# Expert rows in three rounds instead of five parts: tiles that later parts go on filling

## The chip, the cores and the metric

The kernel runs on one core of a Trainium2 chip. The metric is the device time of one execution in microseconds (us). Three timed runs of the kernel before took 2634.92, 2636.18 and 2640.61 us; the median is 2636.18. "Before" is the kernel as it stands, "after" the changed one.

## What is computed

A layer of a graph network (attention over edges), then a layer of a mixture of experts. There are 6250 nodes with 256 features, 206,250 edges sorted by their target, and 16 experts, of which each node uses two. Cut to what matters:

```python
def gnn(x, edge_index, W, a_src, a_dst, gamma, beta):
    hh = (x @ W).reshape(n, 8, 32)
    scores = leaky_relu(s_src[src] + s_dst[dst], 0.2)
    alpha = exp(scores - m[dst]) / denom[dst]
    out = segment_sum(hh[src] * alpha[:, :, None], dst) .reshape(n, 256) + x
    return elu(layernorm(out) * gamma + beta)

def ffn(x, gate_w, gate_b, w1, b1, w2, b2, gamma, beta):
    topk_vals, topk_idx = top_k(x @ gate_w + gate_b, 2)
    topk_w = softmax(topk_vals)
    h = relu(einsum('bsh,ehf->bsef', x, w1) + b1)         # 256 -> 512
    expert_out = einsum('bsef,efh->bseh', h, w2) + b2      # 512 -> 256
    y = x + sum(topk_w * take(expert_out, topk_idx))
    return layernorm(y) * gamma + beta

x = x + gnn(layernorm(x), edges, ...)
x = x + ffn(layernorm(x), ...)
```

## The kernel before, in words

Nodes are cut into 49 blocks of 128, edges into 52 chunks of 31 tiles of 128 edges. A short first stage computes a table row for each node (features, and two exponentials of its scores) and writes it to memory. Then comes one long loop over the 52 chunks, with three kinds of work in it.

*Edges.* A chunk is done in four groups of 8, 8, 8 and 7 edge tiles. GpSimd (POOL in the profile) issues one indirect gather for each edge tile (L188, tile `hx`); `hx` has four buffers, one per group. VectorE (DVE) makes two one-hot tiles (`oh` L864, `ohT` L871), TensorE (PE) fetches the targets' factors with them (`pm`, L879), VectorE weighs the gathered rows (`uv`, L887 to L892, `hx`, L895), and TensorE sums them over the edges (`agg`, L898, 32-bit). At the end of a chunk ScalarE (ACT) copies the sum (`carry`, L912) and stores it (L914). The copies of `carry` therefore mark the chunks in the trace.

*Node blocks.* When a chunk is done, the blocks whose edges are all in are finished by `node_block` (L543): attention output, two layer norms, the row `acc` that goes to the experts, the gate's logits and the top two experts. A table made beforehand says after which chunk a block is due.

*Experts.* The 49 blocks are taken in five parts that end at blocks 14, 26, 35, 43 and 49 (`PARTS`, L30). When the last block of a part is done, at the end of chunks 15, 27, 37, 45 and 51, `part_due` (L823) calls `routing` (L597). Routing counts, with one-hot tiles on VectorE and two matmuls on TensorE (L643, copied out by ScalarE, L644), how many rows each expert gets, rounds each count up to whole tiles of 128, and gives each pair (node, expert) a row (`pos`, L690) and each tile an expert (`owner`, L703). A part of n blocks has 2n + 15 tiles, the most that 2n full tiles of rows can need with 16 experts; that is 43, 39, 33, 31 and 27, together 173. Each part has its own row buffers in memory, `xg` for inputs and `yg` for outputs.

The work of the experts is then spread over the loop: after every group the function `some` (L809) issues at most four scatters of rows (`scatter`, L707, by GpSimd, into `xg`), then one step of biases (`biases`, L719: the gates' shares times `b2`, through TensorE, ScalarE, TensorE and VectorE into `acc`), and moves a pipeline of three tiles one step on: `weights` (L731: read the tile's expert into a register of SyncE, load its rows `xr`, `w1s`, `b1s`), `turned` (L743: load `w2s`, transpose the rows), `hidden` (L754: first matmuls, L758, and relu, L767) and `rows_out` (L770: second matmuls, L773, copy `yr`, L775, store into `yg`, L776). A tile is not begun before all scatters of its part are issued, and its row load waits for all of them. SyncE (SP) issues all the loads in one order, ScalarE the stores. A tile loads 1 MB of weights. `clear` (L534) fills the rows of one part with zeros in each of the first five chunks.

After the loop the tiles that are left are drained, and `result` (L778) gathers each node's two output rows from `yg`, adds them, and writes the result.

A scheduler puts the instructions of all this into one order for each engine; each engine then works through its own order. It does not keep to the order of the program: the 28 scatters of the first part, which the program has after the groups of chunks 16 and 17, stand in one run in GpSimd's order, after the first group of chunk 18's gathers. Small results on TensorE share one PSUM buffer, `pt` in the pool `wk` (`bufs=1`): routing, biases, node blocks and the transposes of the rows all go through it.

Of the kernel before, what the change touches and what calls it, by code (L numbers as in the profile page):

```python
# [20 lines left out]
P = 128  # L21
# [7 lines left out]
SLACK = 24  # L29
PARTS = (14, 26, 35, 43, 49)  # L30


@with_exitstack
def kernel(
# [39 lines left out]
    DUMP = (NB + 1) * P  # L74
    parts = list(zip((0,) + PARTS[:-1], PARTS))
    MTS = [2 * (hi - lo) + E - 1 for lo, hi in parts]
    assert LAST < P and N % P and NE > (NK - 1) * CE and PARTS[-1] == NB

# [8 lines left out]
    accd = dram.tile([(NB + 2) * P, RA], F32, name="accd")  # L87
    xg = [dram.tile([mt * P, C], F32, name=f"xg{i}") for i, mt in enumerate(MTS)]
    yg = [dram.tile([mt * P, C], F32, name=f"yg{i}") for i, mt in enumerate(MTS)]

# [414 lines left out]

    prep.close()


    v8 = const.tile([P, NB, 8], F32, name="v8")
    i8 = const.tile([P, NB, 8], U32, name="i8")  # L510
    nc.vector.tensor_scalar_add(fb, fb, -1.0)
    pos = [const.tile([P, NB], I32, name=f"pos{k}") for k in range(2)]
    gate = [const.tile([P, NB], F32, name=f"gate{k}") for k in range(2)]
    owner = [const.tile([1, mt], I32, name=f"owner{i}") for i, mt in enumerate(MTS)]
    b2r = const.tile([E, C], F32, name="b2r")
    nc.sync.dma_start(b2r, b2)
    tri = const.tile([P, P], F32, name="tri")
    nc.vector.tensor_scalar(tri, irow, nodes[:, 0:1], None, op0=ALU.is_gt)
    mtm = max(MTS)
    jt = const.tile([1, mtm], F32, name="jt")  # L520
    nc.gpsimd.iota(jt, pattern=[[1, mtm]], base=0, channel_multiplier=0, allow_small_or_imprecise_dtypes=True)
    with tc.tile_pool(name="w2", bufs=2) as w2_, tc.tile_pool(name="w3", bufs=3) as w3_, tc.tile_pool(
# [10 lines left out]

        def clear(i):  # L534

            for t in range(0, MTS[i], ZR):
                n = min(ZR, MTS[i] - t)
                nc.sync.dma_start(
                    xg[i][t * P : (t + n) * P, :].rearrange("(p j) c -> p j c", p=P),
                    zero[:, None, :].to_broadcast([P, n, C]),  # L540
                )
# [55 lines left out]
        def routing(i):  # L597

            lo, hi = parts[i]
            nb = hi - lo  # L600
# [51 lines left out]
            if nb > 1:  # L652
                nc.vector.tensor_add(place, place, incl)
                nc.vector.tensor_sub(place, place, own)


            mult = rt.tile([P, nb], F32, name="mult")
            nc.vector.tensor_scalar_mul(mult, irow[:, :nb], float(P))
            gtm = rt.tile([P, E, nb], F32, name="gtm")
            nc.vector.tensor_tensor(  # L660
                gtm,
                incl[:, nb - 1, :].unsqueeze(2).to_broadcast([P, E, nb]),
                mult[:, None, :].to_broadcast([P, E, nb]),
# [6 lines left out]
            while step < E:  # L670
# [4 lines left out]
            tiles_to = cur  # L675
            first_row = rt.tile([P, E], F32, name="first_row")
            nc.vector.tensor_sub(first_row, tiles_to, nt)
            nc.vector.scalar_tensor_tensor(
                place,
                first_row[:, None, :].to_broadcast([P, nb, E]),  # L680
                float(P),
                place,
                op0=ALU.mult,
                op1=ALU.add,
            )
            for k in range(2):
# [5 lines left out]

            mt = MTS[i]
            le = rt.tile([1, mt, E], F32, name="le")
            nc.vector.tensor_tensor(
                le,
                tiles_to[:1, None, :].to_broadcast([1, mt, E]),
                jt[:, :mt, None].to_broadcast([1, mt, E]),
                ALU.is_le,
            )  # L700
            of = rt.tile([1, mt], F32, name="of")
            nc.vector.tensor_reduce(of, le, AX.X, ALU.add)
            nc.vector.tensor_scalar_min(owner[i], of, float(E - 1))  # L703

        scattered = [[] for _ in parts]

        def scatter(i, b, k):  # L707
            n = P if b < NB - 1 else LAST
            t = nc.gpsimd.indirect_dma_start(  # L709
                out=xg[i][:, :],  # L710
                out_offset=bass.IndirectOffsetOnAxis(ap=pos[k][:n, b : b + 1], axis=0),
                in_=acc[:n, b, :],
                in_offset=None,
            )
            for o in scattered[i]:
                tc.declare_no_dep(t.ins, o.ins, reason="each pair has a row of its own")
            scattered[i].append(t)

# [9 lines left out]

        taken = []

        def weights(i, j):  # L731

            after = taken[-3] if len(taken) > 2 else ()
            e = load(owner[i][:, j : j + 1], 0, E - 1, engines=(ET.SP,), after=after)
            xr = e2.tile([P, C], F32, name="xr")
            nc.sync.dma_start(xr, xg[i][j * P : (j + 1) * P, :])
            w1s = e2.tile([P, KC, F], F32, name="w1s")
            nc.sync.dma_start(w1s, w1[ds(e, 1)].rearrange("a (k p) f -> p (a k) f", p=P))
            b1s = e2.tile([P, FC], F32, name="b1s", bufs=3)
            nc.sync.dma_start(b1s, b1d[ds(e, 1)].rearrange("a p f -> (a p) f"))  # L740
            return i, j, e, w1s, b1s, xr
# [28 lines left out]
        def rows_out(i, j, w2s, hT):  # L770
            po = wk.tile([P, C], F32, name="po")
            for f in range(FC):
                nc.tensor.matmul(po, lhsT=hT[:, f, :], rhs=w2s[:, f, :], start=(f == 0), stop=(f == FC - 1))  # L773
            yr = e2.tile([P, C], F32, name="yr")
            nc.scalar.copy(yr, po)  # L775
            nc.scalar.dma_start(yg[i][j * P : (j + 1) * P, :], yr)  # L776

        def result(i, b):  # L778
# [5 lines left out]
            for k in range(2):  # L784
                got = e2.tile([P, C], F32, name=f"got{k}", bufs=3)
                with tc.issue_after(scattered[-1][-1].ins):
                    nc.gpsimd.indirect_dma_start(  # L787
                        out=got[:n],
                        out_offset=None,
                        in_=yg[i][:, :],  # L790
                        in_offset=bass.IndirectOffsetOnAxis(ap=pos[k][:n, b : b + 1], axis=0),
                    )
# [29 lines left out]

        def part_due(i):  # L823
            routing(i)
            lo, hi = parts[i]
            scat.extend((i, b, k) for b in range(lo, hi) for k in range(2))
            bias.extend((i, b) for b in range(lo, hi))
            due.extend((i, j) for j in range(MTS[i]))

# [21 lines left out]
        for k in range(NK):  # L851
# [64 lines left out]
            for b in when.get(k, ()):  # L916
                node_block(b)
                for i, (lo, hi) in enumerate(parts):
                    if b == hi - 1:
                        part_due(i)  # L920
            if k < len(parts):
                clear(k)
        while scat or due or bias or any(at):
            some()
        for i, (lo, hi) in enumerate(parts):
            for b in range(lo, hi):
                result(i, b)
# [33 lines left out]
```

## Time and profile before

| | |
|---|---|
| median of the timed runs | 2636.18 us |
| the profiled execution | 3281.45 us |
| its span, first to last instruction | 3279.4 us |
| mean granted TensorE clock in it | 0.796 |
| moved by DMA | 592.51 MB, mean 181 GB/s |
| first gather to last `carry` | the loop, from about 99 to 2928 us |
| from there to the end | the drain, about 350 us |

The profiled execution is longer than the timed runs; its times are used for shares and for the cost of single steps. A line of a group reads: source line, engine, operation, output<-inputs, count | busy time in us, mean ns of one | idle time of the engine just before them and what ended it. "issue" means that nothing in the profile was waited for, "remote" that the profile cannot name who ended the wait. The ends of matmuls are modelled. A line of stretches reads: begin:end, length, then for each engine the busy time and the number of instructions.

### The profile page before, as it was taken

What the parts mean: (1) busy time and instruction counts of PE and PEld (TensorE: products, weight loads), DVE (VectorE), ACT (ScalarE), POOL (GpSimd) and SP (SyncE); (2) the same over time, 40 slices, a digit from 0 to 9 for tenths busy, and PEclk for the clock granted to TensorE, in tenths of its full rate; (3) what the DMA queues carried; (4) which work ended last, traced back from release to release, by engine and by line L of the source; (5) the groups of instructions that cost most, each with busy time, mean ns of one, the idle gap of its engine ahead of it and who ended that gap; (6) DMA issues with size and microseconds to landing.
All of it is one profiled execution on the core that took longest, in us unless ns stands there. A gap on an engine that the chain in (4) does not pass through costs nothing. (4 is left out here: it accounts for less than half of the span.)

```text
span 3279.4 us, 34441 instructions
## 1 busy us (share of the span) xinstructions
PE 2002.3 (61%) x10215; PEld 1614.8 (49%) x10215; DVE 1585.7 (48%) x3057; ACT 498.2 (15%) x1771; POOL 1759.4 (54%) x1867
## 2 busy tenths in 40 slices
PE   7344445454424877777636677747677657765565
PEld 5233333343323656666525566645466545654454
DVE  6445555465534444554625456445355524544431
ACT  4000000000000211111101111111111111122232
POOL 3665665666675445655555465664455645515501
PEclk9676777777767888888768888977789868887788
DMA  7875443444443657776546667755576746656896
GB/s 189 249 235 157 119 123 109 121 112 121 120 146 112 198 173 213 224 220 211 150 115 192 184 210 213 231 165 174 161 214 207 216 145 194 200 164 212 259 269 203
DMA packets 415255, 592.51 MB, mean 181 GB/s; under 512 B 104295, under 2 KB 304701, under 8 KB 415061
## 3 DMA queue, kind: packets, MB, share of 16 engines
q1 hardware_dynamic: 268968, 276.81, 28.5%
q0 software_dynamic: 89904, 263.85, 27.8%
q10 hardware_dynamic: 56188, 49.56, 4.4%
q8 instruction: 84, 1.38, 0.2%
q14 instruction: 111, 0.90, 0.1%
HBM read 504.00 MB, written 86.02 MB: 180 GB/s over the span
## 5 line engine op out<-in xcount | busy, mean ns | idle before, releaser
L188 POOL DMA_INDIRECT hx<-table,src_sb x1612 | 1537.3, 954 | 1153.8 <-issue 432.3
L898 PE MATMUL agg<-hx,oh 128*128 128x264 f32 x3224 | 977.3, 462 | 382.1 <-DVE hx L895 222.2
L898 PEld LDWEIGHTS agg<-hx,oh 128*128 128x128 f32 x3224 | 719.8, 231 | 552.1 <-DVE hx L895 233.8
L773 PE MATMUL po<-w2s,hT 128*128 128x256 f32 x1384 | 414.5, 444 | 252.3 <-ACT hT L767 194.6
L887 DVE TENSOR_REDUCE uv<-pm 128x128 f32<-128x384 f32 x208 | 112.2, 539 | 785.2 <-remote 340.0
L895 DVE TENSOR_TENSOR hx<-hx,pm 128x2112 f32<-128x2112 f32 x208 | 474.5, 2281 | 3.4
L773 PEld LDWEIGHTS po<-w2s,hT 128*128 128x128 f32 x1384 | 283.3, 218 | 319.8 <-ACT hT L767 211.9
L758 PEld LDWEIGHTS ph<-xt,w1s 128*128 128x128 f32 x2768 | 368.0, 206 | 44.6 <-issue 27.2
L758 PE MATMUL ph<-xt,w1s 128*128 128x128 f32 x2768 | 377.7, 291 | 12.5 <-issue 7.0
L767 ACT ACTIVATE hT<-ph,b1s 128x128 f32<-128x128 f32 x692 | 198.1, 368 | 634.3 <-remote 259.3
L864 DVE TENSOR_TENSOR oh<-along,dl 128x1024 f32<-128x1024 f32 x208 | 245.3, 1179 | 48.9 <-remote 28.8
L871 DVE TENSOR_TENSOR ohT<-dlr,along 128x1024 bf16<-128x1024 uint8 x208 | 244.8, 1177 | 5.7 <-DMA dlr<-dlb 5.7
L879 PE MATMUL pm<-abw,ohT 128*128 128x48 bf16 x1612 | 88.3, 187 | 237.7 <-DVE ohT L871 143.6
L879 PEld LDWEIGHTS <-ohT 128*128 128x128 bf16 x1612 | 77.4, 99 | 275.7 <-DVE ohT L871 168.6
L787 POOL DMA_INDIRECT got<-yg,pos x98 | 97.4, 994 | 197.0 <-DMA yg<-yr 130.7
L709 POOL DMA_INDIRECT xg<-acc,pos x98 | 96.1, 981 | 94.4 <-DVE pf L689 61.8
L775 ACT COPY yr<-po 128x256 f32<-128x256 f32 x173 | 64.1, 370 | 422.9 <-PE agg L898 107.3
L180 ACT ACTIVATE mv<-mv,eps 128x1 f32<-128x1 f32 x98 | 28.8, 294 | 645.5 <-DVE mv L177 237.4
L589 PE MATMUL pt<-gw,yt 128*128 128x16 f32 x196 | 37.3, 306 | 107.9 <-ACT yt L586 75.0
L727 DVE TENSOR_TENSOR acc<-acc,pt 128x256 f32<-128x256 f32 x49 | 20.5, 418 | 169.9 <-PE pt L726 107.3
L589 PEld LDWEIGHTS pt<-gw,yt 128*128 128x128 f32 x196 | 33.0, 238 | 122.4 <-ACT yt L586 85.6
L793 DVE SCALAR_TENSOR_TENSOR acc<-got,gate,acc 128x256 f32<-128x256 f32 (+1 forms) x98 | 45.3, 474 | 94.2 <-DMA got<-yg,pos 89.2
(185 smaller groups left out, 1314.7 us busy)
## 6 DMA issues: line engine op xcount, KB each, us to landing
w1s<-in_L_ffn_w_dram SPq DMA_DIRECT2D x173, 512.0 KB
w2s<-in_L_ffn_w_dram SPq DMA_DIRECT2D x173, 512.0 KB
hx<-table,src_sb POOLq DMA_INDIRECT x1612
dlr<-dlb SPq DMA_DIRECT2D x52, 496.0 KB
xr<-xg SPq DMA_DIRECT2D x173, 128.0 KB
yg<-yr ACTq DMA_DIRECT2D x173, 128.0 KB
xg<-zero SPq DMA_DIRECT2D x19, 1024.0 KB
accd<-carry ACTq DMA_DIRECT2D x52, 132.0 KB
```

What stands on the lines that cost most here:

```text
L188: t = nc.gpsimd.indirect_dma_start(out=hx[:, g, :], out_offset=None, in_=table[:, :], in_offset=bass.IndirectOffsetOnAxis(ap=src_sb[:, c : ...
L709: t = nc.gpsimd.indirect_dma_start(out=xg[i][:, :], out_offset=bass.IndirectOffsetOnAxis(ap=pos[k][:n, b : b + 1], axis=0), in_=acc[:n, b, :],
L758: nc.tensor.matmul(ph[:, f, :], lhsT=w1s[:, k, f * P : (f + 1) * P], rhs=xt[:, k, :], start=(k == 0), stop=(k == KC - 1),)
L767: nc.scalar.activation(hT[:, f, :], ph[:, f, :], AF.Relu, bias=b1s[:, f : f + 1])
L773: nc.tensor.matmul(po, lhsT=hT[:, f, :], rhs=w2s[:, f, :], start=(f == 0), stop=(f == FC - 1))
L787: nc.gpsimd.indirect_dma_start(out=got[:n], out_offset=None, in_=yg[i][:, :], in_offset=bass.IndirectOffsetOnAxis(ap=pos[k][:n, b : b + 1] ...
L864: nc.vector.tensor_tensor(oh, along[:, None, :P].to_broadcast([P, n, P]), dl[:, t0 + g0 : t0 + g0 + n, None].to_broadcast([P, n, P]), ALU. ...
L871: nc.vector.tensor_tensor(ohT, dlr[:, g0 : g0 + n, :], along[:, None, P:].to_broadcast([P, n, P]), ALU.is_equal,)
L879: nc.tensor.matmul(pm[:, g * S3 : (g + 1) * S3], lhsT=ohT[:, g, :], rhs=abw, start=True, stop=True)
L887: nc.vector.tensor_reduce(uv, pm[:, : n * S3].rearrange("p (n t h) -> p n h t", n=n, t=3), AX.X, ALU.add)
L895: nc.vector.tensor_tensor(rows, rows, wt.unsqueeze(3).to_broadcast([P, n, H, D1]), ALU.mult)
L898: nc.tensor.matmul(agg, lhsT=oh[:, g, :], rhs=hx[:, g, :RA], start=(g0 == 0 and g == 0), stop=(carry is None and g0 + g == CT - 1),)
```

## The change

There are three rounds, which end at blocks 36, 43 and 49. The first is routed in eight parts that end at blocks 10, 14, 18, 22, 26, 30, 34 and 36; the other two rounds are one part each. Within a round the parts go on in one another's tiles: routing keeps, from part to part, the count of rows of each expert, where its open tile stands (`here`, `edge`), how many tiles are opened, and to whom each belongs (`whose`). Rows that still fit go into the expert's open tile, the others into new ones. Only tiles that are full are due after a part; how many are taken is fixed beforehand, as the least number of full tiles there must be by then: 5, then 8 after each of the next six parts. The last part of the round takes the remaining 34. With one remainder for each round instead of each part the tiles are 87 + 29 + 27 = 143. The parts of the first round fall due at the end of chunks 10, 15, 19, 23, 27, 32, 36 and 38, the other rounds at 45 and 51.

Since tiles that are due need not lie in a row, routing makes a list of them (`page`), by ranking the flags with a matmul and by selecting with two more (first rows, owners). SyncE then reads a second register for each of the 87 tiles of the first round, and so does ScalarE, for the address of the output. The three row buffers are shared by the parts of a round, and declarations say that a tile taken earlier isn't touched by later scatters. The lists of small tiles move from the pool `const` to a pool `late`, opened after the first stage's pool is closed.

Core of the diff:

```diff
-PARTS = (14, 26, 35, 43, 49)
+ROUNDS = ((10, 14, 18, 22, 26, 30, 34, 36), (43,), (49,))
...
+    PAGES = [2 * (hi - lo) + E - 1 for lo, hi in zip(begins, ends)]
+    parts = []
+    for r, cuts in enumerate(ROUNDS):
+        lo, done = begins[r], 0
+        for hi in cuts:
+            n = PAGES[r] if hi == cuts[-1] else max(0, 2 * (hi - begins[r]) - E + 1)
+            parts.append((lo, hi, r, hi == cuts[-1], n - done))
+            lo, done = hi, n
...
+            if begin:
+                for t in (count, edge, here, opened):
+                    nc.vector.memset(t, 0.0)
+            else:
+                nc.vector.tensor_tensor(place, place, count[:, None, :].to_broadcast([P, nb, E]), ALU.add)
+            nc.vector.tensor_add(count, count, incl[:, nb - 1, :])
+            over = rt.tile([P, E], F32, name="over")
+            nc.vector.tensor_sub(over, count, edge)
...
+            nc.vector.tensor_scalar(tiles_to, tiles_to, opened, None, op0=ALU.add)
+            there = rt.tile([P, E], F32, name="there")
+            nc.vector.tensor_sub(there, tiles_to, nt)
+            nc.vector.scalar_tensor_tensor(there, there, float(P), edge, op0=ALU.mult, op1=ALU.subtract)
...
+                jump = rt.tile([P, E], F32, name="jump")
+                nc.vector.tensor_sub(jump, there, here)
+                beyond = rt.tile([P, nb, E], F32, name="tot0")
+                nc.vector.tensor_tensor(beyond, place, edge[:, None, :].to_broadcast([P, nb, E]), ALU.is_ge)
+                nc.vector.tensor_tensor(beyond, beyond, jump[:, None, :].to_broadcast([P, nb, E]), ALU.mult)
+                nc.vector.tensor_tensor(place, place, here[:, None, :].to_broadcast([P, nb, E]), ALU.add)
+                nc.vector.tensor_add(place, place, beyond)
...
+                    nc.vector.tensor_mul(le, of, count)
+                    nc.vector.tensor_reduce(due_now, le, AX.X, ALU.add)
+                    nc.vector.scalar_tensor_tensor(
+                        due_now, due_now, full_at, was_due, op0=ALU.is_ge, op1=ALU.subtract
+                    )
+                pr = wk.tile([P, 1], F32, name="pt")
+                nc.tensor.matmul(pr, lhsT=tri, rhs=due_now, start=True, stop=True)
+                rank = rt.tile([P, 1], F32, name="rank")
+                nc.vector.tensor_copy(rank, pr)
+                take = rt.tile([P, mt], F32, name="take")
+                nc.vector.tensor_scalar(take, irow[:, :mt], rank, due_now, op0=ALU.is_equal, op1=ALU.mult)
...
+                pp = wk.tile([1, mt], F32, name="pt")
+                nc.tensor.matmul(pp, lhsT=first_row, rhs=take, start=True, stop=True)
+                nc.vector.tensor_copy(page[i], pp)
...
+            po = wk.tile([1, mt], F32, name="pt")
+            nc.tensor.matmul(po, lhsT=whose, rhs=take, start=True, stop=True)
+            nc.vector.tensor_scalar_min(owner[i], po, float(E - 1))
...
             e = load(owner[i][:, j : j + 1], 0, E - 1, engines=(ET.SP,), after=after)
+            row = j * P
+            if parts[i][-1] < PAGES[r]:
+                row = load(page[i][:, j : j + 1], 0, (PAGES[r] - 1) * P, engines=(ET.SP,), after=after)
             xr = e2.tile([P, C], F32, name="xr")
-            nc.sync.dma_start(xr, xg[i][j * P : (j + 1) * P, :])
+            t = nc.sync.dma_start(xr, xg[r][ds(row, P), :])
...
             nc.scalar.copy(yr, po)
-            nc.scalar.dma_start(yg[i][j * P : (j + 1) * P, :], yr)
+            r = parts[i][2]
+            row = j * P
+            if parts[i][-1] < PAGES[r]:
+                row = load(
+                    page[i][:, j : j + 1], 0, (PAGES[r] - 1) * P, engines=(ET.Activation,), after=stored[-1:]
+                )
+            t = nc.scalar.dma_start(yg[r][ds(row, P), :], yr)
...
-            if k < len(parts):
+            if k < len(ROUNDS):
                 clear(k)
```

## The prediction

> **What bounds the kernel now.** I read the page first, then stretches of time, then the waits. The page gives the span and four engines between 48 and 61%, none of them full:
>
> ```profile
> span 3279.4 us, 34441 instructions
> PE 2002.3 (61%) x10215; PEld 1614.8 (49%) x10215; DVE 1585.7 (48%) x3057; ACT 498.2 (15%) x1771; POOL 1759.4 (54%) x1867
> PEclk9676777777767888888768888977789868887788
> L188 POOL DMA_INDIRECT hx<-table,src_sb x1612 | 1537.3, 954 | 1153.8 <-issue 432.3
> L709 POOL DMA_INDIRECT xg<-acc,pos x98 | 96.1, 981 | 94.4 <-DVE pf L689 61.8
> ```
>
> A share over the span mixes stages, so I cut the span at the copies of `carry` (L912), one per chunk of 31 edge tiles, and counted in each stretch the chunks (L912), expert tiles (`yr`, L775), scatters (L709) and bias steps (L726). Columns: stretch, length, busy time of PE, PEld, DVE, ACT and POOL, granted clock, DMA share, GB/s.
>
> ```profile
> 209.50:924.00 714.50, 326.90 (x1504) 255.07 (x1502) 382.75 (x638) 30.87 (x100) 451.33 (x472) 0.72 0.46 128
> 924.00:1202.80 278.80, 160.28 (x770) 125.67 (x771) 115.50 (x215) 34.20 (x116) 151.70 (x159) 0.74 0.54 158
> 1202.80:1550.00 347.20, 265.13 (x1422) 218.50 (x1422) 185.78 (x301) 64.90 (x217) 203.38 (x214) 0.88 0.71 216
> 1550.00:1928.00 378.00, 231.32 (x1158) 184.89 (x1158) 168.17 (x298) 50.84 (x171) 198.38 (x209) 0.78 0.55 161
> 1928.00:2122.80 194.80, 148.55 (x823) 122.87 (x822) 106.28 (x173) 36.82 (x124) 118.58 (x125) 0.90 0.74 224
> 2122.80:2441.00 318.20, 206.25 (x1058) 166.12 (x1057) 143.80 (x268) 49.37 (x167) 164.73 (x173) 0.79 0.59 176
> 2589.00:2788.60 199.60, 124.88 (x656) 100.15 (x654) 83.21 (x157) 28.73 (x98) 108.50 (x115) 0.79 0.60 178
> 2929.00:3279.40 350.40, 206.36 (x1098) 169.95 (x1096) 125.65 (x377) 100.08 (x365) 110.17 (x110) 0.80 0.75 229
> ```
>
> Three readings. The first row is 15 chunks with no expert tile: 714.5/15 = 47.6 us each. The third and fifth are 7 and 4 chunks with four tiles each: 49.6 and 48.7, so about 49. Four tiles cost a chunk about 1.4 us: in the loop a tile is nearly free. The second, fourth, sixth and seventh rows hold 4, 6, 5 and 3 chunks and each one routing; at 49 a chunk they are 82.8, 84.0, 73.2 and 52.6 us too long, 293 us in all. That is what the parts cost, and they hold 86 scatters and 43 bias steps. The last row is the drain.
>
> I split the 293. POOL issues the scatters in one run with 0.30 us between them, 28 from 943.3 to 978.4, so 1.25 us each: 86 x 1.25 = 107. The chunks that hold a routing without a run of scatters (those that end at 1609.4, 2181.0 and 2650.4) took 60.3, 59.2 and 62.4, so about 11 above 49: four routings, 44. The remaining 142 I put on 43 bias steps, 3.3 each. How the waits look:
>
> ```profile
> PEld agg L898 <- DVE hx L895: 233.8, 56, 23.0
> POOL hx L188 <- PE agg L898: 181.3, 28, 16.9
> DVE acc L727 <- PE pt L726: 107.3, 22, 28.7
> ACT yr L775 <- PE agg L898: 107.3, 17, 8.0
> ```
>
> The reader is to see that POOL waits for the matmuls to free a gathered tile, the matmuls for VectorE, and VectorE for small matmuls that stand in PE's order: a loop of latencies through four buffers, and no full engine.
>
> **What the Trainium skill says.** "TensorE: Matmul & The Clock Gate", Part 1 (the HAM clock gate): the array runs at half clock unless it is kept busy. The trace agrees: 0.72 without tiles, 0.88 and 0.90 with four a chunk. This speaks for cheap tiles: they keep the clock up for the edge matmuls. "VectorE: DVE Perf Modes", the section on the TRN2 errata: an operation pays a fixed time however small it is. Agrees: the 128x15 sums of L673 took 164 ns, while the 128x192 of L649 took 354, 13 times the elements at twice the time. "DMA: Bandwidth & Descriptors", "Issuing engines are not separate DMA queues": DMAs of all issuers share 16 engines. No run here isolates it; the DMA share in the tile stretches is 0.71 to 0.74, so that fewer weights need not shorten them.
>
> **The change part by part**, in the profiled time. Scheduling can be read from the built programs without times: after the last edge matmul 41 tiles are left on PE in both.
>
> 1. Tiles: 173 become 143 (87 + 29 + 27). All 30 fall in the loop. In the row above four tiles cost 1.4 us, so 30/4 x 1.4 = 10 us off. Their 30 MB of weights and 7.5 MB of rows fall in stretches where DMA is 0.7 busy. Bounds: nothing, and all of PE's time, 30 x 4.46 = 134 (4.46 is the distance of tiles in the drain: the first `po` matmuls at 3200.93 and 3205.39). I take 10.
>
> 2. Routings in the loop: four become nine (the last stays in the drain). At the measured 11 each, 5 x 11 = 55 more. With it goes, each time, the trip of `place` and `own` through PE and ACT (L643, L644): one PE buffer, so that the second matmul stands 12.2 us behind the copy of the first in the routing at 912. VectorE waits meanwhile, and behind it its one-hots and products, and then POOL for buffers.
>
> 3. VectorE operations: the built order has 170 in the four routings of the loop and 581 in the nine. At some 0.19 each (0.16 to 0.17 for the small ones, 0.38 only for 14 blocks) 110 us; nine routings at the before's 45/4 = 11.3 (12.7, 12.1, 10.5 and 9.7 measured) are 101. So 9 more.
>
> 4. New round trips through PE: the due flags' rank, the page rows and the owners, three in eight routings. They stand in a row on PE right after the next group's 48-wide matmuls, before the biases and the tiles, which wait behind them on PE; VectorE waits for each. No row shows them. The nearest is L643, 0.4 to 0.6 us on PE, with a copy and the wake-ups I take 0.8: 24 x 0.8 = 19. Bounds: 0 where PE is backlogged anyway, and 24 x 4 = 96 if each waits for half a group of edge matmuls at low clock (the 12-us wait at 912 is a whole one).
>
> 5. Scatters: 98 in both, no run put in front of work that it waits for longer than now. But the long runs of 28, 24 and 18 become 20, then six of 8 and one of 4. POOL needs 31 x 1.25 = 38.8 of a 47.6-us chunk, so a chunk without tiles has 8.9 spare, and each short run is followed by two of them. A run of 28 stalls the four buffers at full price; of the short ones' 52 x 1.25 = 65 I take half as hidden, 32 off. Bounds: 0 and 65.
>
> 6. A second register load per tile on SP and one on ACT, for 87 tiles. No view shows one; the nearest is an ACT DMA issue, 0.33 us. ACT is 15% busy and the next tile's `hT` waits behind: I take 5 us, bounds 0 and 87 x 0.33 = 29. On SP the tile's rows and weights and the chunk's `dlr`, `abw`, `a` and `xb` stand behind; `dlr` and `abw` are fetched two chunks early and SP only issues, so I take nothing; uncovered, another 29.
>
> 7. Clearing: 173 pages to 143 and in three chunks rather than five, 11 MB of it at chunk 0. DMA is under half busy there: nothing, bounds -10 and +10. Biases: 43 in the loop as before, nothing. The drain: the same 41 tiles, 12 scatters and 98 gathers, and a last round of the same six blocks: nothing.
>
> Sum: -10 + 55 + 9 + 19 - 32 + 5 = +46 us on 3281.45. The profiled execution took 3281.45 us (span 3279.4 and 2.05 around it), the median of the runs shown is 2636.18: 0.803 of it. I scale differences by this, for want of a profile of a shorter run: +46 becomes +37, so **2673 us**.
>
> **The rivals.** *Tiles count after all (faster).* The timed runs are 645 us shorter than the profiled one, so the waits that hide a tile may be gone there, and each tile then costs PE's 4.46. For: PE is busy 76% in the tile stretches, and PE's records understate it. Against: the tile-free chunk is no faster in the profile. -134 + 83 - 32 + 5 = -78, scaled -63: 2573. It decides when a tile costs more than (83 - 32 + 5)/30 = 1.9 us instead of 0.35. *Routings are hidden.* The new ones fall in tile-free stretches where PE is behind at half clock anyway (0.72), and steps 2 and 4 come to about 40 rather than 74: total +12, about 2646; if 30 they cancel, 2638. For: in the chunk at 1010.4, with routing and 28 scatters, only 4 us are left beyond scatters. *Each routing is a full stall.* Three PE trips at the upper bound and no scatter hidden: -10 + 55 + 9 + 96 + 5 = +155, scaled +124: 2760. *The change doesn't cut tiles*: excluded, the built program holds 143.
>
> **How the numbers follow.** Forecast 0.54; tiles count 0.25 (2573, from 2540 to 2630); routings hidden 0.11 (2638 to 2646); full stall 0.10 (2760). From 2590 to 2735 the forecast's own spread, the hidden case and a part of both outer ones are held. A measurement of this kernel can tell 0.2%, some 5 us, from no change: faster 0.30 (tiles count 0.25, the lower edge of the others 0.05), same 0.08, slower 0.62.
>
> **What would show it.** Right: 102 tiles in the loop and 42 after the last `carry`; chunks without tiles still near 48, with four near 49; each of the seven routings from chunk 12 to 39 followed by an excess of some 30 to 40 us; the drain near 350. Step 2 is wrong if the chunks with a routing stand under 52; step 4 if PE's waits before the rank matmul are under 1 us or over 4; step 5 if POOL's short runs add their full 10 us. The forecast is wrong if tile-free chunks fall clearly below 45 while those with tiles stay at 49: then tiles had a price.

## The result, and the profile after

The changed kernel takes 2816.6 us (median of 4 runs, 2814.41 to 2820.76), the kernel before beside it 2638.39 (4 runs, 2634.92 to 2644.17): ratio 1.0675, 95% interval 1.0651 to 1.0699. It is slower, as forecast, but by 178 us instead of 37, above the 2590 to 2735 us that the prediction gave as its range.

To read what follows, one has to know that the kernel before ran at 2635 to 2638 us in most sets of runs and at 3277 to 3281 in two sets, each on another chip, and that the profiled execution of the prediction (3281.45 us) is of the second kind, so that the lines of before below come from a repeat of it (2634.08 us, the first experiment).

The page of the kernel after: span, busy time by engine, granted clock, and three of the costliest groups (busy time, mean ns of one | idle time ahead of them, and what ended most of it).

```profile
span 2814.9 us, 33324 instructions
PE 1842.8 (65%) x9507; PEld 1480.1 (53%) x9507; DVE 1606.7 (57%) x3479; ACT 447.1 (16%) x1606; POOL 1765.1 (63%) x1866
PEclk9777777867877968969869769868898989977898
L199 POOL DMA_INDIRECT hx<-table,src_sb x1612 | 1543.8, 958 | 714.4 <-issue 416.1
L820 DVE TENSOR_TENSOR acc<-acc,pt 128x256 f32<-128x256 f32 x49 | 20.6, 420 | 298.1 <-DMA xg<-acc,pos 191.8
L800 POOL DMA_INDIRECT xg<-acc,pos x98 | 95.8, 978 | 90.2 <-DVE pf L728 60.6
```

The new line is the second: the 49 additions of the biases are 20.6 us of work, but VectorE stood idle 298 us ahead of them, 192 of it until a scatter (`xg<-acc,pos`) had read the rows that they overwrite. The busy times of the five engines tell nothing of this: POOL's is 1765 us against 1766 in the repeat of before, VectorE's 1607 against 1585.

Stretches between copies of `carry`, with the columns of the table in the prediction. First the repeat of before: 7 chunks without tiles, 4 with four tiles each, and the drain.

```profile
504.40:780.60 276.20, 168.28 (x709) 127.31 (x709) 179.38 (x294) 13.54 (x44) 209.49 (x220) 0.80 0.50 139
1032.10:1195.90 163.80, 135.76 (x820) 117.74 (x819) 105.35 (x173) 36.47 (x124) 118.24 (x124) 0.92 0.83 262
2313.20:2632.20 319.00, 200.29 (x1104) 166.72 (x1102) 125.67 (x377) 100.36 (x367) 111.55 (x110) 0.85 0.79 252
```

Then after: twice four chunks with one short part in them, four chunks with tiles (14 in all) and no routing, and the drain.

```profile
809.20:1002.70 193.50, 121.81 (x634) 97.45 (x634) 112.36 (x245) 24.63 (x84) 127.13 (x133) 0.81 0.61 174
1002.70:1194.90 192.20, 119.61 (x634) 95.69 (x634) 112.71 (x244) 24.62 (x84) 125.08 (x132) 0.80 0.60 175
2102.30:2262.20 159.90, 130.34 (x751) 111.14 (x751) 106.37 (x193) 32.17 (x111) 113.94 (x120) 0.88 0.81 253
2490.20:2814.90 324.70, 198.42 (x1106) 164.69 (x1104) 127.28 (x381) 100.17 (x367) 110.13 (x110) 0.84 0.79 248
```

An ordinary chunk takes 276.2/7 = 39.5 us without tiles and 163.8/4 = 41.0 with four, and about the same in after (159.9/4 = 40.0). That is POOL's own pace: in the first of these lines it is busy 209.5 us in 220 instructions, and with the 0.30 us that it leaves ahead of each (as in its timeline below) that makes 275.5 of the 276.2 us. Per chunk, 31 gathers at 1.25 us are 38.8. Four chunks with a short part take 193 us where four plain ones and 8 scatters would take 4 x 39.5 + 10 = 168. The drain is 6 us longer (324.7 against 319). So the loop is what changed: the last `carry` comes at 2490.2 instead of 2313.2.

Which waits are new? Of the waits of after (total, times, longest):

```profile
DVE acc L820 <- DMA xg<-acc,pos: 191.8, 11, 24.5
POOL hx L199 <- PE agg L1011: 189.2, 78, 24.5
PE pt L815 <- DVE acc L820: 156.6, 7, 24.7
PE pt L851 <- DMA xr<-xg: 64.5, 10, 18.9
```

and the same wait of POOL in the repeat of before:

```profile
POOL hx L188 <- PE agg L898: 14.0, 46, 0.3
```

In before POOL never waited for the edge matmuls longer than its usual 0.3 us between two instructions. In after it did once per short part, for 24 us in each of the six parts with 8 scatters. Adding up POOL's waits of over 1 us, from the fourth chunk's gathers to the last gather, gives 42 us in before and 220.5 in after: 178 more, and the loop is 177 longer. Here, where POOL sets the pace, its waits are the whole bill.

How one of these comes about, from the timeline of after (start, duration, instruction, and in brackets the idle time before it). VectorE's lines that touch `acc`:

```profile
835.74 0.40 DVE L602 TENSOR_SCALAR acc<-xb,mv 128x256 f32<-128x256 f32 x1
860.67 0.42 DVE L820 TENSOR_TENSOR acc<-acc,pt 128x256 f32<-128x256 f32 x1 [24.52 <-DMA xg<-acc,pos]
```

PE's line that waits for that addition, because it needs the single `pt` buffer:

```profile
861.14 0.38 PE L815 MATMUL pt<-ident,gs 128*16 128x128 f32 x1 [24.68 <-DVE acc L820]
```

and POOL's first, second and last scatter of the part, and the gather that paid for it:

```profile
856.82 1.00 POOL L800 DMA_INDIRECT xg<-acc,pos  x1 [0.30 <-issue]
858.12 0.98 POOL L800 DMA_INDIRECT xg<-acc,pos  x1 [0.30 <-issue]
...
865.73 0.96 POOL L800 DMA_INDIRECT xg<-acc,pos  x1 [0.30 <-issue]
891.03 0.98 POOL L199 DMA_INDIRECT hx<-table,src_sb  x1 [24.33 <-PE agg L1011]
```

At 836 VectorE comes to the first bias addition. It may not overwrite these rows of `acc` before the two scatters that read them are done, but those stand on POOL behind two more groups of gathers and are issued from 856.8 on. For 24.5 us VectorE does nothing, PE behind it neither; the edge products that stand behind the addition on VectorE are late, buffers come free late, and POOL, once its 8 scatters are out, waits 24.3 us for them. It waits at once, because by then it is four groups of gathers ahead of VectorE and all four buffers of `hx` are taken. The Trainium skill, "PSUM — Partial Sum Buffer", section "Engine vs sequencer instructions", says that the queues of VectorE and GpSimd are strictly first in, first out. The trace agrees: no edge product of VectorE overtakes the addition that waits from 836 to 860.

### The profile page after: what moved, and what is told of

Same layout as the page of the kernel before. It is cut to its first block, busy times and chain, and to the rows that moved or that the text cites. A ratio compares the mean times of both kernels' runs of the same rounds, so it can differ in the third digit from the quotient of the medians.

```text
span 2814.9 us, 33324 instructions
## 1 busy us (share of the span) xinstructions
PE 1842.8 (65%) x9507; PEld 1480.1 (53%) x9507; DVE 1606.7 (57%) x3479; ACT 447.1 (16%) x1606; POOL 1765.1 (63%) x1866
## 5 line engine op out<-in xcount | busy, mean ns | idle before, releaser
L1011 PE MATMUL agg<-hx,oh 128*128 128x264 f32 x3224 | 994.3, 469 | 336.0 <-DVE hx L1008 335.6
L1011 PEld LDWEIGHTS agg<-hx,oh 128*128 128x128 f32 x3224 | 733.4, 236 | 515.1 <-DVE hx L1008 363.8
L875 PE MATMUL po<-w2s,hT 128*128 128x256 f32 x1144 | 303.7, 404 | 58.8 <-ACT hT L869 56.3
L860 PEld LDWEIGHTS ph<-xt,w1s 128*128 128x128 f32 x2288 | 298.1, 204 | 32.9 <-issue 13.4
L860 PE MATMUL ph<-xt,w1s 128*128 128x128 f32 x2288 | 307.7, 289 | 9.2 <-DMA w1s<-in_L_ffn_w_dram 4.6
L875 PEld LDWEIGHTS po<-w2s,hT 128*128 128x128 f32 x1144 | 213.9, 199 | 102.0 <-ACT hT L869 73.5
L1003 DVE TENSOR_TENSOR uv<-uv,hx 128x128 f32<-128x128 f32 x208 | 59.3, 285 | 277.3 <-DMA hx<-table,src_sb 218.4
L869 ACT ACTIVATE hT<-ph,b1s 128x128 f32<-128x128 f32 x572 | 163.2, 367 | 278.4 <-PE ph L860 218.6
L820 DVE TENSOR_TENSOR acc<-acc,pt 128x256 f32<-128x256 f32 x49 | 20.6, 420 | 298.1 <-DMA xg<-acc,pos 191.8
L851 PE MATMUL pt<-ident,xr 128*128 128x128 f32 x286 | 60.2, 294 | 97.1 <-DMA xr<-xg 64.5
L815 PE MATMUL pt<-ident,gs 128*16 128x128 f32 x49 | 16.1, 328 | 162.0 <-DVE acc L820 156.6
```

Source lines behind the costliest of these rows:

```text
L860: nc.tensor.matmul(ph[:, f, :], lhsT=w1s[:, k, f * P : (f + 1) * P], rhs=xt[:, k, :], start=(k == 0), stop=(k == KC - 1),)
L869: nc.scalar.activation(hT[:, f, :], ph[:, f, :], AF.Relu, bias=b1s[:, f : f + 1])
L1011: nc.tensor.matmul(agg, lhsT=oh[:, g, :], rhs=hx[:, g, :RA], start=(g0 == 0 and g == 0), stop=(carry is None and g0 + g == CT - 1),)
```

## The experiments

Times are in us. Each ratio is to the kernel before in the same set of runs, which takes 2635 to 2636 us where nothing else is said. Theory: VectorE and PE reach work of a part before POOL has issued the scatters on which that work waits, and a run of 8 scatters is too short to hide it. Main rival: the new code of the routing (trips through PE, more VectorE operations, two register loads a tile) is itself the cost.

**The kernel before, again** (2634.08).

> The kernel before, unchanged, for a second profile. In the profile of after (2814.9 us of span, 2816.6 timed) chunks without a routing take 35 to 41 us, while the first profile of before had 47 to 50 (3279 us of span, 2636 timed). If the first profile was of an execution that was slow throughout, this one has a span near 2634 and plain chunks near 40 us. If profiling itself slows this kernel, it is near 3280 again.

It gave the lines of before above, and one more thing. The same wait exists in before:

```profile
827.26 0.42 DVE L727 TENSOR_TENSOR acc<-acc,pt 128x256 f32<-128x256 f32 x1 [19.93 <-DMA xg<-acc,pos]
```

but POOL doesn't feel it: its 28 scatters run from 815.9 to 851.0, 24 us of them after VectorE has gone on, in which VectorE and PE catch up, and the next gather follows at once.

```profile
850.08 0.96 POOL L709 DMA_INDIRECT xg<-acc,pos  x1 [0.30 <-issue]
851.35 0.98 POOL L188 DMA_INDIRECT hx<-table,src_sb  x1 [0.30 <-issue]
```

**Biases late.** Each part's bias steps begin eight steps (two chunks) after its routing.

```diff
-            if bias and not scat:
+            step_no[0] += 1
+            if bias and not scat and step_no[0] > bias_from[bias[0][0]]:
...
+            bias_from[i] = step_no[0] + 8
```

> The changed kernel with the bias steps of a part begun eight steps after its routing, instead of as soon as its scatters are issued. Theory A (the first bias add of a part waits on VectorE for the scatter of the same rows, 24 us in each of eight parts, and that alone is the loss): near 2640 us, 2620 to 2680. Theory B (the tiles wait for the same scatters on TensorE: their first transposes stand a chunk ahead of the scatters too, so the stall only changes its place): 2770 or more. Theory C (nine routings instead of four, by their VectorE operations and TensorE trips): 2780 or more.

2758.99, ratio 1.0467 (1.045 to 1.0485), 58 us less than the changed kernel: far from theory A, and nearest to theory B (2770 or more). The chunks with a short part still take 85 to 90 us. The wait moved on to the transposes of the tiles' rows, which stand behind the same scatters:

```profile
PE pt L851 <- DMA xr<-xg: 208.5, 15, 30.7
```

**Biases and tiles late.** The same delay for the part's tiles (six steps for the seventh part).

```diff
-            if due and not any(t[0] == due[0][0] for t in scat):
+            if due and step_no[0] > bias_from[due[0][0]] and not any(t[0] == due[0][0] for t in scat):
```

> The changed kernel with both the bias steps and the tiles of a part begun eight steps after its routing (six for the seventh part). In the built order neither then stands ahead of the scatters. Theories A and B (what stands in the order ahead of the scatters that it waits for): 2600 to 2670 us, with POOL's 24-us waits gone. Theory C (the routings themselves): 2760 or more, with chunks of a routing still 30 us or more above the others.

2669.83, ratio 1.0137 (1.012 to 1.0154). As theories A and B had it, POOL's wait for the edge matmuls is nearly gone, and the loop ends at 2320.7, 7.5 us after that of before. The rest is in the drain, which has 49 tiles instead of 42. The delay wasn't all that moved: in this built order the scatters of four of the six parts with 8 scatters also stand one group of gathers earlier on POOL.

```profile
POOL hx L199 <- PE agg L1015: 29.2, 59, 10.4
```

**The old five parts in the new code.** `ROUNDS = ((14,), (26,), (35,), (43,), (49,))`.

> The changed kernel's code with the five old parts, each as a round of its own (173 tiles, four routings in the loop). Theories A and B: the distances are again nearly those of before, so 2630 to 2680 us. Theory C in the form that the new routing code is dear by itself: 2700 or more; in the form that only the number of routings counts: near 2640 as well.

2656.59, ratio 1.0101 (1.0067 to 1.0135), so 21 us for the new code with five parts. Its loop ends at 2331.7 (18.5 later than in before) and POOL waits 15.6 us more there. That is within what theories A and B expected, and under the 2700 of a dear new code.

**The short parts in the old code.** Ten parts, old routing, no row registers:

```diff
-PARTS = (14, 26, 35, 43, 49)
+PARTS = (10, 14, 18, 22, 26, 30, 34, 36, 43, 49)
...
+    DONE = [5, 8, 8, 8, 8, 8, 23, 19, 29, 27]
...
-            due.extend((i, j) for j in range(MTS[i]))
+            due.extend((i, j) for j in range(DONE[i]))
```

> The kernel before with its old routing, old tiles (every part has pages of its own) and no register load of a row, cut into the ten parts of the changed kernel, and with as many tiles due per part as there (5, five times 8, 23, 19, 29, 27; 143 in all). It leaves out the other 105 tiles that ten separate parts would need and fills their output rows with zeros. Scatters, biases and tiles stand where they stand in the changed kernel, within a quarter of a chunk. Theory A (the order costs: VectorE and PE wait for a scatter, and a run of 8 scatters is too short to hide it): almost the whole loss without any of the new code, 2770 to 2810 us, with chunks of 85 to 95 us at the eight short parts. Theory B (the new code costs: three more trips through PE, new VectorE operations, a row register per tile): 2640 to 2690 us and routing chunks under 65.

2737.96, ratio 1.0387 (1.0365 to 1.0409): below theory A's window, far above theory B's. With none of the new code, its chunks with a short part take 84 to 86 us. In the built order its scatters stand one group of gathers earlier than in the changed kernel, and POOL's wait per part is 14 to 16 us instead of 24, although VectorE's wait is as long as there:

```profile
854.75 0.42 DVE L734 TENSOR_TENSOR acc<-acc,pt 128x256 f32<-128x256 f32 x1 [24.32 <-DMA xg<-acc,pos]
880.52 0.95 POOL L189 DMA_INDIRECT hx<-table,src_sb  x1 [14.49 <-PE agg L905]
```

So the place of the scatters on POOL counts in a second way. With them a group earlier, one of the four buffers is still free, and POOL issues seven more gathers after its last scatter before it has to wait. In before the first part's scatters stand at the same place, but there are 28 of them and POOL doesn't wait: this is what a long run is worth.

**24 tiles fewer.** The kernel before with 12 tiles less in parts one and two: `DONE = [mt - (12 if i < 2 else 0) for i, mt in enumerate(MTS)]`.

> The kernel before without the last 12 tiles of each of its first two parts; their output rows are filled with zeros instead. All 24 stood in the loop over the edges. If a tile in the loop is nearly free, as chunks with four tiles (40.8 us) against chunks with none (39.2) say, 24 x 0.4 = 10 us go: 2626. If a tile costs what it costs PE, 4.3 each as in the drain, 103 us go: 2533. If it is free, 2636.

2630.37, ratio 0.9984 (0.9973 to 0.9996): 5 us for 24 tiles, 0.2 each. A tile beside the edges is nearly free.

**Late, but not the last parts.** `due_from[i] = bias_from[i] if i < 8 else 0`.

> The changed kernel with the biases and tiles of the first round's parts begun eight steps after their routing, as in the run before it, but the tiles of the two later parts begun at once. That run had 49 tiles after the last carry where the kernel before has 42, and its drain was 346 us where that of the kernel before is 319; its loop was only 7.5 us longer. Theory A: those seven tiles are most of what was left: 2670 - 27 = 2643. Theory B (the new code is what was left): 2665 to 2670.

2672.48, ratio 1.0136 (1.0116 to 1.0157). The edit freed nothing: tiles start in the order of the parts, so that the later parts still stood behind the delayed ones and 49 tiles were again left. It doesn't tell the theories apart.

**Fewer cuts.** The run just above with `ROUNDS = ((16, 26, 34, 36), (43,), (49,))`.

> The run of late biases and tiles, last parts at once, with the first round cut in four (blocks up to 16, 26, 34, 36) instead of eight: 143 tiles as in the changed kernel, five routings in the loop instead of nine. Theory A: a cut still costs some 5 us for its routing (VectorE and the trips), so about 20 us less than the run with eight cuts, 2620 to 2630, and faster than the kernel before. Theory B: with the stall gone a cut is free and the longer runs of scatters gain nothing: the same as the run with eight cuts, within 5 us.

2730.13, ratio 1.0359 (1.0339 to 1.0379): both expectations missed. 55 tiles are left after the last `carry` and the drain takes 379 us, 60 more than in before; the loop ends 33 later. Since the drain grows by 27 us with 7 more tiles and by 60 with 13, a tile costs some 4 to 4.6 us there and 0.2 in the loop: starting tiles late isn't free.

**Scatters earlier.** The changed kernel with the scatters moved on POOL and nothing else edited (the built order of VectorE and PE differs in a few places only, by some instructions): gathers that come eight steps (or nine) after a part's routing are queued behind its last scatter.

```diff
-                hx, gathered = early.pop(0) if k == 0 else gather(k, g0, n)
+                with ExitStack() as order:
+                    if due_at and step_no[0] >= due_at[-1] + 8:
+                        order.enter_context(tc.issue_after(scattered[parts[len(due_at) - 1][2]][-1][1].ins))
+                    hx, gathered = early.pop(0) if k == 0 else gather(k, g0, n)
```

First beside a kernel before of 3281.23 us:

> The changed kernel, whole, with one thing moved: on POOL the scatters of each part stand two groups of gathers (half a chunk) earlier, at once behind the gathers during which the routing ends. Biases, tiles and the routing stay where they were, and nothing is left out. Theory A (the place of the scatters): the scatters issue 20 us earlier, POOL's wait of 24 us per part for the matmuls shrinks to some 4, 8 x 20 = 160 us go: 2657, and routing chunks are near 73 instead of 93. Theory B (what the new routing does on VectorE and PE is the stall): 2800 to 2817.

> The same with half the dose: the scatters of each part stand one group of gathers (10 us) earlier, where they also stand in the run with the old code and short parts. Theory A: 8 x 10 = 80 us go: 2737, equal to that run (2738) within 10 us, and routing chunks are near 83. If what is left in that run came from the new code instead of from this group: 2790 to 2817.

3387.16, ratio 1.0335 (1.0293 to 1.0378), and 3385.22, ratio 1.0327 (1.0277 to 1.0376). What the changed kernel itself takes there was measured beside a kernel before of 3277.02 us:

> The changed kernel, unaltered, beside the runs that follow. On a chip where the kernel before takes 2636 us: 2817, ratio 1.0675. On a chip where it takes 3281 us and POOL already waits in every chunk: if the stall is a wait that POOL's lost time pays for, less of it shows, and the ratio is about that of the runs with earlier scatters there, 1.03 to 1.05.

The change costs 1.025 there (1.0181 to 1.0318; 3369.93), a little under what was expected, and the two moves 1.0369 (1.0304 to 1.0435) and 1.0293 (1.0207 to 1.0378): on such a chip the place of the scatters gains nothing. Then beside a kernel before of 2634.97 us:

> The changed kernel with the scatters of each part half a chunk earlier on POOL, nothing left out. Where the kernel before takes 2636 us: theory A (place of the scatters) 2657, routing chunks near 73 instead of 93; theory B (new code) 2800 to 2817. Where the kernel before takes 3281: ratio near 1.035 once more, which tells nothing.

2691.3, ratio 1.0209 (1.0189 to 1.0229): 125 of the 178 us are gone with the place of the scatters. That is 34 us above theory A's 2657, which counted 20 us for each of eight parts: the first part, with 20 scatters, had no wait of POOL to lose, and the sixth of the later ones didn't move. Of the seven later cuts of the first round, the first five have chunks of 70 to 74 us instead of 93. The sixth is a control that came unasked: there the built order kept the scatters where they were, and its chunk is 93.5 us as in the changed kernel. (The seventh, of 4 scatters, and the first part moved by one group.) POOL's gathers after the scatters of one moved part, and of that one:

```profile
865.05 0.94 POOL L199 DMA_INDIRECT hx<-table,src_sb  x1 [4.71 <-PE agg L1020]
...
1790.50 0.98 POOL L199 DMA_INDIRECT hx<-table,src_sb  x1 [24.15 <-PE agg L1020]
```

and VectorE's wait at the moved one, with the scatters issued from 830.5 on instead of 856.8:

```profile
834.30 0.42 DVE L820 TENSOR_TENSOR acc<-acc,pt 128x256 f32<-128x256 f32 x1 [4.47 <-DMA xg<-acc,pos]
```

The move by one group wasn't measured beside a kernel before of 2635 us.

**A fifth tile a chunk**, in the kernel before (`if k > 20: some()` after each chunk's store), as a way to shorten the drain.

> The kernel before with a fifth step per chunk from chunk 21 on, so that a tile can start five times a chunk instead of four. 34 tiles instead of 42 are left after the last carry. Theory A (a tile beside the edges costs 0.2 us, one in the drain 4.3): the drain gets 8 x 4.3 = 34 us shorter and the loop stays: 2602. Theory B (DMA at 0.84 and PE at 0.83 of the time in chunks with four tiles have no room for a fifth): the loop gets as much longer as the drain gets shorter, 2636 or more.

> The kernel before with a fifth step per chunk from chunk 21 on. Where it takes 2636 us: theory A (there is room beside the edges) 2602, the drain 34 us shorter and the loop as long; theory B (no room) 2636 or more. Where it takes 3281: ratio near 1.014 once more.

3324.04, 1.0131 (1.0079 to 1.0183), and 1.0144 (1.0107 to 1.0181) in the next set, against 3281 and 3277; against 2634.97 it is 2696.9, 1.0222 (1.0198 to 1.0245). Theory B. Four chunks with five tiles each, and the drain, in the last of these:

```profile
1535.10:1712.80 177.70, 153.19 (x926) 132.76 (x925) 105.13 (x172) 43.70 (x150) 118.43 (x125) 0.92 0.84 273
2412.50:2696.60 284.10, 172.04 (x922) 143.15 (x920) 125.65 (x377) 86.56 (x325) 110.72 (x110) 0.82 0.79 251
```

The drain is 35 us shorter, as expected, but a chunk takes 44.4 us instead of 41.0 and the loop ends 99 us later. The fifth tile costs 3.4 us where the first four cost 1.5 together. Which of PE and DMA has no room wasn't separated.

**Both together** in the changed kernel:

> The changed kernel with the scatters half a chunk earlier and a fifth step per chunk from chunk 41 on: 32 tiles instead of 42 in the drain. Theory A for both: 2657 - 10 x 4.3 = 2614, faster than the kernel before. If the fifth tile finds no room: 2657. If the place of the scatters isn't the cause: 2775 or more.

3388.81, 1.0342 (1.0294 to 1.0391), against 3281.23; it wasn't measured beside a kernel before of 2635 us. No version tried that does all the work is faster than the kernel before.

Over all the runs beside a kernel before of 2635 to 2638 us, POOL's waits and the loop go together, whatever was edited (us; waits of over 1 us as counted above):

| kernel | POOL's waits | last `carry` at | tiles left then | drain | median |
|---|---|---|---|---|---|
| before, again | 42 | 2313 | 42 | 319 | 2634 |
| changed | 221 | 2490 | 42 | 325 | 2817 |
| biases late | 179 | 2444 | 42 | 314 | 2759 |
| biases and tiles late | 53 | 2321 | 49 | 346 | 2670 |
| old parts, new code | 58 | 2332 | 42 | 321 | 2657 |
| short parts, old code | 151 | 2424 | 42 | 320 | 2738 |
| 24 tiles fewer | 39 | 2309 | 42 | 313 | 2630 |
| late, not the last parts | 54 | 2324 | 49 | 347 | 2672 |
| late, fewer cuts | 67 | 2346 | 55 | 379 | 2730 |
| scatters earlier | 94 | 2362 | 42 | 327 | 2691 |
| before, five tiles | 150 | 2413 | 35 | 284 | 2697 |

Take POOL's waits off the time of the last `carry`, and 2263 to 2279 us are left in every row, with four routings in the loop or nine, old code or new. So whatever the routings cost, it shows, to within these 16 us, only as far as it makes POOL wait. The granted clock is no rival: its mean is 0.859 in before, 0.817 in the changed kernel and 0.828 with biases and tiles late, where the loop is nearly as short as in before.

## Why the prediction was right in sign and far too small

**The step that failed is step 5**, "no run put in front of work that it waits for longer than now", and with it step 7's "Biases: 43 in the loop as before, nothing". Step 5 asked only what POOL waits for. It didn't ask who waits for POOL: the bias additions on VectorE and the tiles' transposes on PE wait for the scatters' reads and writes, and both stood ahead of them: 24.5 us of VectorE's time, and 24 of POOL's, in each of six parts. Moving the scatters by half a chunk took 125 us off; delaying biases and tiles took 147 off (2816.6 - 2669.8), though 27 were given back in the drain.

**Half hidden, the other half of step 5**, went the wrong way. The prediction gave each plain chunk "8.9 spare" on POOL and took 32 us off because short runs would use it. In the runs that count a plain chunk is 39.5 us and POOL needs 38.8: nothing is spare, and a scatter costs its 1.25 us in any run. What a long run has is cover: 35 us of scatters hid VectorE's wait of 20, and 10 us don't hide one of 24.5. Splitting took cover away, and with the new routing a free buffer too. Instead of -32 the term is about +178 by POOL's waits.

**The sign was luck.** It came from steps 2, 3 and 4 (83 us), which outweighed what tiles and hidden scatters were to save. With the stall out of the way (biases and tiles late) nine routings and the new code leave the loop only 7.5 us longer. That this run's 2670 us are close to the forecast's 2673 is chance as well: 27 of its 34 us are the tiles that start late and end up in the drain.

**What bounds the kernel** was read from an execution of the other kind. "A loop of latencies through four buffers, and no full engine" is true of it: POOL's waits add up to 691 us there. In the repeat, which is like the runs that were timed, they are 42, and POOL is the full engine of the loop, although its busy share is 67% on the page, since the 0.30 us between two instructions aren't counted and the drain is. Scaling by 0.803 couldn't repair that. From the `carry` of chunk 11 to the last, beyond 39.5 us a chunk, before has 2313.2 - 583.8 - 40 x 39.5 = 149 us, of which 86 scatters at 1.26 are 108; the prediction's 293 become 235 when scaled, 114 of it (142 x 0.803) for bias steps that cost next to nothing there. After has 2490.2 - 583.5 - 1580 = 327, where the forecast's 293 + 46 are 272 when scaled. So more than half of the 141 us by which the forecast fell short lies in the price that it read for the parts of before. Even on the other kind of chip the change costs 93 us (3369.93 - 3277.02), twice the forecast's +46 in that time.

**Step 1** was right: 101 tiles are copied out in the loop and 42 after the last `carry` (the prediction's 102 and 42 are one more than its 143), and a tile is worth 0.2 us (24 tiles, 5 us) against the forecast's 0.35; the rival "tiles count" is out.

**Steps 2, 3, 4 and 6** (routings, their operations, trips, register loads; 88 us together) weren't measured one by one. All the new code with five parts costs 21 us, 15.6 of it in POOL's waits. In the short parts the changed kernel takes 79 us more than the old code (2816.6 - 2738.0), but there its scatters also stand one group later; two groups were worth 125, so one is about 60 and some 20 is left for the new code, an estimate from these three runs. Of step 4, PE's waits ahead of the three new matmuls in the routing at 832 were 4.05, 0.92 and 0.25 us, 5.2 together against the 2.4 taken: the first just over the 4 us that were to call the step wrong, and still no stall. Step 2's sign, routing chunks under 52 us, didn't come: they take 62 to 94, but by the stall and the scatters.

**Step 7**, the drain: 324.7 against 319, nearly nothing, as said.

**Of the signs to look for**, "tile-free chunks fall clearly below 45" came true, but those with four tiles fell too (39.5 and 41.0), so that tiles got no price. "POOL's short runs add their full 10 us" came true, and was the smaller part. An "excess of some 30 to 40 us" after each routing came true too (193.5 - 158 = 35.5, and 34), but made of 10 us of scatters and 25 of stall. Of the rivals, "each routing is a full stall" (2760) had the right shape, a stall per part, by the wrong mechanism: not PE's trips but a scatter that is late.

**What stays open**: why the built order puts the scatters a group later with the new routing than with the old; what of the new code costs the remaining 20 us; and why this kernel is slower on two of the chips, and gains nothing there from earlier scatters.

## What to carry to other kernels

When a transfer or its issue is moved or regrouped, look up in the built order of every engine what waits for it, a write that may not overtake its read included, and whether it stands ahead of it. Here a wait of VectorE, which wasn't the bound, was paid for by POOL, which was, as soon as POOL's buffers were used up. A long run on the bounding engine may be the cover of somebody else's wait: before you split it, look for what catches up meanwhile. And before costing anything from a profile, compare its own time with the timed runs: when it is 24% longer, its bound may be another one, and a scale factor doesn't bring it back.

## What the runs showed of the hardware

The same program took 2635 to 2638 us on some chips and 3277 to 3281 on two others, with a mean granted clock of 0.859 and 0.796 in the profiles. In the experiments each chip was used for one set only, so the runs don't tell whether it is the chip or the time; nor do they tell whether the clock is the cause. POOL waits 42 us for others in the one and 691 in the other. On one of the two others POOL's waits in the changed kernel look like this (the first line is its usual gap between two instructions), and a change worth 1.0675 is worth 1.025:

```profile
POOL hx L199 <- issue: 432.9, 1418, 1.2
POOL hx L199 <- PE agg L1011: 407.2, 53, 27.6
POOL hx L199 <- PE pm L992: 144.7, 20, 17.8
```

Its waits add up to 790 us, 99 more than in before (691), and its span is 101 longer (3380.4 against 3279.4): the same account holds there.

Two more figures. In the lines above a gather or scatter holds POOL for 0.94 to 1.00 us, with 0.30 us ahead of it where nothing is waited for, so one takes about 1.25 us. And VectorE went on about 2.5 us after POOL began to issue the second of the two scatters that read its rows (858.12 to 860.67; 831.76 to 834.30 when moved).
